# Layer 2's context keys: turned by VectorE in 32x32 blocks and stored in runs of 32 keys, instead of transposed by TensorE

## The chip, the cores and the metric

The kernel runs on one core of one Trainium2 chip. Four compute engines work beside each other, each on its own list of instructions, in order: TensorE (PE in the profile; its weight loads are a second row, PEld), VectorE (DVE), ScalarE (ACT) and GpSimd (POOL). A fifth, SyncE (SP), issues most of the transfers; ScalarE and GpSimd issue some too. All transfers share 16 DMA engines. Work tiles lie in on-chip memory of 128 partitions; TensorE writes its products to a small accumulator memory (PSUM), from which VectorE or ScalarE must copy them.

The metric is the device time of one launch in microseconds (us). Three runs of the kernel before the change took 2389.08, 2390.23 and 2396.24 us; the median is 2390.23.

## The reference, cut to what matters

Four layers, each a cross attention over a context and a feed-forward block, are applied to x of shape 4 x 256 x 256; the context has 4 x 1601 x 256 numbers. The change lies in layer 2's attention, with 16 query heads and 4 key/value heads of 128 numbers:

```python
q = rms_norm((x @ wq).reshape(B, L, 16, 128), q_norm_w)
k = rms_norm((x @ wk).reshape(B, L, 4, 128), k_norm_w)
k_ctx = rms_norm((h_ctx_kv @ wk_ctx).reshape(B, T, 4, 128), k_norm_w)
v_ctx = (h_ctx_kv @ wv_ctx).reshape(B, T, 4, 128)
...
k_full = jnp.concatenate([k_ctx, k], axis=1)
scores = jnp.einsum('blhd,bmhd->bhlm', q, k_full) * scale + mask
probs = jax.nn.softmax(scores, axis=-1)
```

For each of 4 batches and 4 key/value heads, which makes 16 units, 1601 context keys and values are computed from the context, the keys are divided by their root mean square and multiplied by a weight of 128 numbers, and the scores need them turned: the 128 numbers of a key on partitions, the keys side by side. These keys and values do not depend on x.

## The kernel before, in words

**The early pieces.** Because layer 2's context keys and values do not depend on x, they are computed during layers 0 and 1, in pieces that a generator (`l2_early`, L1272) hands out. `fill(n)` (L174) asks for n pieces, at places where TensorE would otherwise wait for a router's small operations or for gathered rows. A unit has seven product pieces (`products`, L1295): two blocks of 128 context rows each, multiplied by a 256 x 256 weight (keys and values at once), copied by ScalarE from the accumulator into `kr_early` (keys) and `va_early` (values, seven buffers), the values sent to device memory (`vd`, L1316) from SP. Every other piece ScalarE squares four blocks of keys and VectorE sums the squares (L1325, L1326). After the seventh, `norm` (L1328) multiplies the unit's keys by the reciprocal root, four operations of up to 512 columns, on GpSimd, or on VectorE while `self.scaler` is set to it (in the adds of layers 0 and 1, where GpSimd is gathering).

Then follow, for the unit before it, four turn pieces (`turns`, L1336): up to four 128x128 transposes by TensorE into the accumulator, one ScalarE copy that multiplies by the key weight (there a column, one number per partition) into `kT_early`, and one transfer from SP to `kd` in device memory, laid out as 128 partitions x 13 blocks x 128 keys. In all 16 x 7 + 16 x 4 = 176 pieces.

**Where they are asked for.** Three in layer 0's attention; `F0` in layer 0's router (L410 on); `G0` nine times in layer 0's adds (`l0_add`, L608); `F1` before layer 1's feed-forward; `G1` in layer 1's adds (L959 on); `LN2`, `Q2`, `C2` while layer 2's first unit is prepared (L1670 on); what is left is then drawn at once. In layer 0's adds GpSimd gathers, for each of eight groups of tokens, eight tiles of expert outputs (L630) into 24 buffers; VectorE adds each, scaled, to x (L622, in written order), and after every second group runs layer 1's small attention (`l1_xattn`).

**What sets the order.** The program is written as one sequence; a planner then orders each engine's list by priority and its own estimates of durations, keeps the dependencies with semaphores and frees buffers. `pin` (and `mm` while `strict` is set) keeps an instruction in written order. At run time each engine, and SP with its transfers, takes its list strictly in order, so an instruction that waits holds up all behind it.

**Layer 2's attention.** The early tiles' memory (`e2`) is freed and used by the attention's probabilities (`p2`, eight buffers) and turned probabilities (`pT2`). `prep` (L1452) loads a unit's keys and values from `kd` and `vd` a unit ahead and adds the 256 own keys. The scores of 32 queries (`scores`, L1549) are made as four matmuls beside each other, one for each 32 of the 128 array columns: matmul a takes keys 32a to 32a+31 of every block, so before the change it reads 32 keys, skips 96, and so on. That lets VectorE turn the probabilities in 32x32 blocks (L1613).

Layer 3 already has keys in such runs: `l3_spread` (L1841) turns them by VectorE and sends them by four transfers.

## Time and profile before

| | us |
|---|---|
| median of three runs | 2390.23 |
| the profiled execution | 2387.69 |
| its span, first to last instruction | 2386.0 |
| TensorE busy | 2255.6 |
| VectorE busy | 1473.2 |
| ScalarE busy | 1272.4 |
| GpSimd busy | 948.7 |

The profile is of one execution. A group is all instructions of one line, engine and shape: its busy time, the mean duration in ns, then the time for which its engine stood idle just before them, with what ended that. "issue" is a wait that the profile can lay to nothing. Matmuls follow each other in a pipeline, so a mean duration is longer than the step from one to the next, and each fp32 product is recorded as two matmuls. The granted clock is TensorE's share of full speed. A wait is laid to what ended last.

The places of the early pieces in that execution: layer 0's attention to 121 us, its router to 208, its experts to 364, its adds (with layer 1's first pieces) to 510, layer 1's feed-forward to 619, its adds to 653, the preparation of layer 2 to 692, then layer 2's attention to 1700.

### The profile page before, as it was taken

The page shows a single profiled execution, that of the slowest core. Times are in us where ns is not written, and L with a number is a line of the kernel's source. Part 1 is how long each engine was busy: PE and PEld are TensorE (multiplying, and loading weights), DVE is VectorE, ACT ScalarE, POOL GpSimd, SP SyncE. Part 2 cuts the span into 40 slices and gives each one's busy share as a digit, 9 for nine tenths or more (in the row PEclk, how much of TensorE's full clock was granted, in tenths as well). Part 3 has the DMA queues.
Part 4 walks back from the last instruction along what each step waited for, and adds up shares of the span by engine and source line. Part 5 has one row for each costly group of instructions (what it writes and reads, how often), then busy time and mean ns, then how long its engine had stood idle before and what let it go on. Part 6 is the DMA issues. An engine that isn't in the chain of part 4 may idle for free.

```text
span 2386.0 us, 42230 instructions
## 1 busy us (share of the span) xinstructions
PE 2255.6 (95%) x14335; PEld 1382.2 (58%) x14335; DVE 1473.2 (62%) x3553; ACT 1272.4 (53%) x2877; POOL 948.7 (40%) x1707
## 2 busy tenths in 40 slices
PE   8989997889989999999999999999899889999996
PEld 5677875777745555555555655555665533444332
DVE  5453532773457777777777777777334574758344
ACT  3334443552474555555555555553232577888994
POOL 1014655503335544555554555554121253334220
PEclk9989998989999999999999999999899999999998
DMA  7165575652550111111111111100534353434320
GB/s 267 41 201 161 172 156 157 197 185 65 167 179 32 43 51 47 47 51 51 51 52 51 51 51 50 44 10 10 205 124 117 114 156 103 109 94 103 83 64 19
DMA packets 156078, 234.47 MB, mean 98 GB/s; under 512 B 33929, under 2 KB 122761, under 8 KB 154666
## 3 DMA queue, kind: packets, MB, share of 16 engines
q1 hardware_dynamic: 138998, 190.07, 25.0%
q0 software_dynamic: 11280, 31.60, 5.4%
q10 hardware_dynamic: 5588, 10.09, 1.4%
q8 instruction: 117, 1.92, 0.3%
q14 instruction: 95, 0.78, 0.1%
HBM read 169.94 MB, written 61.74 MB: 97 GB/s over the span
## 4 chain that ended last, share of the span: by engine, by line
PE 78%; DVE 7%; issue 5%; DMA 4%; ACT 2%; POOL 2%; SPq 1%; ACTq 0%; POOLq 0%; DVEq 0%
PE o L117 17%; PE s L117 17%; PE o L77 6%; PE b L77 3%; PE f2gu L117 3%; PE s L77 3%; PE f1gu L117 2%; PE fill L1307 2%; PE f0gu L117 2%; PE acc L117 2%; PE tpq L117 2%; PE av L117 2%; PE f0y L117 2%; PE f2y L117 1%; PE f1y L117 1%
## 5 line engine op out<-in xcount | busy, mean ns | idle before, releaser
L1572 ACT ACTIVATE p<-s,nmsm 128x448 f32<-128x448 f32 (+2 forms) x512 | 324.7, 639 | 369.6 <-DVE nmsm L1567 317.4
L117 PE MATMUL o<-pT,va 128*128 128x256 f32 (+2 forms) x1920 | 431.7, 377 | 3.3 <-DVE pT L1613 2.9
L117 PE MATMUL s<-kT,qT 128*32 128x448 f32 (+2 forms) x4096 | 424.2, 550 | 4.2 <-ACT p L1572 4.2
L77 ACT ACTIVATE e<-s 128x1024 f32<-128x1024 f32 (+1 forms) x416 | 392.4, 1041 | 57.4 <-PE s L77 56.3
L117 PEld LDWEIGHTS o<-pT,va 128*128 128x128 f32 (+1 forms) x1920 | 344.7, 190 | 127.9 <-issue 75.4
L1607 POOL TENSOR_SCALAR p<-p,rm 128x448 f32<-128x448 f32 (+2 forms) x512 | 320.7, 649 | 6.3
L1567 DVE TENSOR_REDUCE nmsm<-s 128x1 f32<-128x448 f32 (+4 forms) x384 | 293.2, 783 | 4.4
L1613 DVE STREAM_TRANSPOSE pT<-p 128x448 f32<-128x448 f32 (+4 forms) x384 | 278.1, 778 | 11.1 <-POOL p L1607 11.1
L117 PEld LDWEIGHTS s<-kT,qT 128*32 128x32 f32 x4096 | 121.7, 109 | 250.2 <-issue 213.9
L77 PE MATMUL o<-e,va 128*32 128x512 f32 x1656 | 246.9, 614 | 12.3 <-DVE os L77 12.2
L1600 POOL TENSOR_TENSOR rm<-em,tot 32x8 f32<-32x8 f32 x256 | 50.3, 197 | 335.6 <-DVE tot L1597 303.3
L1564 DVE TENSOR_TENSOR s<-s,mask 128x64 f32<-128x64 f32 (+4 forms) x384 | 92.5, 260 | 128.5 <-PE s L117 82.4
L77 PEld LDWEIGHTS s<-qb,kb 32*128 32x128 f32 (+1 forms) x1664 | 65.5, 180 | 182.3 <-issue 143.7
L1307 PE MATMUL fill<-wkc_early,ctxT 128*128 128x256 f32 (+1 forms) x444 | 110.5, 401 | 8.9 <-ACT va_early L1315 6.7
L522 POOL DMA_INDIRECT f0xr<-f0xd,f0src x95 | 91.3, 961 | 66.5 <-PE f0y L117 25.5
L77 PE MATMUL s<-qb,kb 32*128 32x256 f32 (+1 forms) x1664 | 111.5, 331 | 3.1 <-ACT e L77 1.8
L77 POOL CAST kb<-kf 128x384 fp32r<-128x384 f32 (+1 forms) x126 | 65.5, 549 | 96.4 <-PE s L77 61.8
L1307 PEld LDWEIGHTS fill<-wkc_early,ctxT 128*128 128x128 f32 (+1 forms) x444 | 87.0, 200 | 25.3 <-ACT va_early L1315 7.8
L1572 ACT ACTIVATION_READ_ACCUMULATOR p<-s,nmsm 128x1 f32 x512 | 100.5, 196 | 0.0
L1326 DVE TENSOR_REDUCE ss_early<-sq_early 128x4 f32<-128x512 f32 x64 | 37.1, 580 | 82.8 <-ACT sq_early L1325 72.0
L630 POOL DMA_INDIRECT f0yt<-f0yd,f0slot x64 | 63.1, 987 | 60.7 <-DVE x L622 29.8
L117 PE MATMUL f2gu<-f2wgu,f2xsT 128*128 x176 | 85.1, 608 | 0.6 <-ACT f2xsT L114 0.3
(579 smaller groups left out, 3689.2 us busy)
## 6 DMA issues: line engine op xcount, KB each, us to landing
kf<-kd SPq DMA_DIRECT2D x384, 48.0 KB
vd<-va_early SPq DMA_DIRECT2D x96, 128.0 KB
kd<-kT_early SPq DMA_DIRECT2D x48, 256.0 KB
kT<-kd SPq DMA_DIRECT2D x16, 768.0 KB
va<-vd SPq DMA_DIRECT2D x16, 768.0 KB
kd<-kt SPq DMA_DIRECT2D x96, 128.0 KB
f0yd<-f0ys SPq DMA_DIRECT2D x95, 128.0 KB
ctxT<-in_ctxT SPq DMA_DIRECT2D x5, 1664.0 KB
```

What stands on the lines that cost most here:

```text
L77: ins = f(*a, **kw)
L117: self.ordered(self.nc.tensor.matmul(out, lhsT, rhs, start=start, stop=stop, **kw))
L522: nc.gpsimd.indirect_dma_start(out=t, out_offset=None, in_=xd[:, :], in_offset=bass.IndirectOffsetOnAxis(ap=src[:, n : n + 1], axis=0),)
L630: nc.gpsimd.indirect_dma_start(out=yt, out_offset=None, in_=yd[:, :], in_offset=bass.IndirectOffsetOnAxis(ap=slot[:, t, r : r + 1], axis=0),)
L1307: ins = nc.tensor.matmul(tp[:rows, t, :], ctxT[u // NKV2][:, k, c0 : c0 + rows], w[u % NKV2][:, k, :], start=k == 0, stop=k == 1,)
L1326: nc.vector.tensor_reduce(ss[:, m0:m1], sq[:, : m1 - m0, :], AX.X, ALU.add)
L1564: nc.vector.tensor_tensor(sv, sv, mask[:, e0:e1, : nt - CT, :].rearrange("p n t i -> p n (t i)"), ALU.add)
L1567: nc.vector.tensor_reduce(ms[:, 0, e0:e1], s[:, n0:n1, : nt * 32], AX.X, ALU.max, negate=True)
L1572: nc.scalar.activation(p[:, n, : nt * 32], s[:, n, : nt * 32], AF.Exp, bias=ms[:, 0, e : e + 1], accum_out=ms[:, 1, e : e + 1],)
L1600: nc.gpsimd.tensor_tensor(r[32 * a : 32 * a + 32], e[:, a], tot, ALU.mult)
L1607: nc.gpsimd.tensor_scalar(p[:, n, : nt * 32], p[:, n, : nt * 32], r[:, e : e + 1], 1.0, ALU.mult, ALU.mult)
L1613: self.pin(nc.vector.transpose(pT[:, 2 * c + n0 : 2 * c + n1, :nt, :].rearrange("p n t i -> p n (t i)"), p[:, n0:n1, : nt * 32],))
```

## The change

- The keys are no longer transposed by TensorE. `turn` lets VectorE transpose 32x32 blocks of up to five key blocks at a time (`TURNS2`: blocks 0-3, 4-7, 8-12), straight from `kr_early` into `kT_early` (now three buffers). A 32x32 transpose leaves each group of 32 numbers of a key on the partitions of its own group of 32 keys; four transfers a turn, each from 32 partitions, put the pieces where they belong.
- In device memory and on chip the keys now lie as 128 partitions x 4 groups x 13 blocks x 32 keys, so that matmul a of the scores reads one unbroken run.
- The key weight is now a row over 128 numbers on all partitions; it is multiplied in `norm`. On VectorE that is one fused instruction for each of 13 blocks; on GpSimd it is a second pass, in all six operations.
- The turns are no pieces of their own: those of the unit before go into products 3, 4 and 5 of the next unit. That leaves 112 pieces, and `F0`, `G0`, `F1`, `G1` and `C2` ask for fewer.
- The own keys of a unit go into the new layout by two copies instead of one.

```diff
@@ -45,12 +45,13 @@
 CT2 = NM - 1
 
 
-F0 = [0, 0, 0, 0, 6, 8, 4, 4]
-G0 = 9
+F0 = [0, 0, 0, 0, 5, 6, 3, 3]
+G0 = 5
 REGS = 4
-F1 = [1, 2, 2, 3]
-G1 = [7, 4, 4, 3, 2, 2, 2, 2, 2, 2, 0]
-LN2, Q2, C2 = 2, 2, 6
+F1 = [1, 1, 2, 2]
+G1 = [5, 3, 3, 2, 2, 2, 2, 1, 1, 1, 0]
+LN2, Q2, C2 = 2, 2, 4
+TURNS2 = ((0, 4), (4, 8), (8, NM))
 FIRST3 = [7, 1, 3]
 EARLY = B * NKV2
 NH3, HD3 = 32, 8
@@ -1277,14 +1278,18 @@
         nc, tc, i = self.nc, self.tc, self.i
         e2 = self.e2
         self.scaler = nc.gpsimd
-        kw = self.const.tile([P, 1], F32, name="kw_early")
-        nc.sync.dma_start(kw, i["l2_knw"].rearrange("o p -> p o"))
+        kw = e2.tile([P, HD2], F32, name="kw_early")
+        nc.sync.dma_start(kw, i["l2_knw"].to_broadcast([P, HD2]))
         w = []
         for g in range(NKV2):
             w.append(e2.tile([P, 2, 256], F32, name="wkc_early", bufs=NKV2))
             nc.sync.dma_start(w[g], i["l2_wkc"][g])
         self.early_kv = [
-            [self.dram.tile([P, NM, HD2], F32, name=f"{n}{u}", bufs=1) for n in ("kd2", "vd2")] for u in range(EARLY)
+            (
+                self.dram.tile([P, 4, NM, 32], F32, name=f"kd2{u}", bufs=1),
+                self.dram.tile([P, NM, HD2], F32, name=f"vd2{u}", bufs=1),
+            )
+            for u in range(EARLY)
         ]
 
 
@@ -1327,33 +1332,42 @@
 
         def norm(kr, ss):
             self.rstd(ss, ss, 1.0 / HD2, self.eps6)
-            for m in range(0, NM, 4):
-                n = min(4, NM - m)
-                self.scaler.tensor_tensor(
-                    kr[:, m : m + n, :], kr[:, m : m + n, :], ss[:, m : m + n, None].to_broadcast([P, n, HD2]), ALU.mult
+            if self.scaler is nc.vector:
+                for m in range(NM):
+                    nc.vector.scalar_tensor_tensor(kr[:, m, :], kr[:, m, :], ss[:, m : m + 1], kw, ALU.mult, ALU.mult)
+                return
+            for m0, m1 in TURNS2:
+                to = [P, m1 - m0, HD2]
+                for by in (ss[:, m0:m1, None].to_broadcast(to), kw[:, None, :].to_broadcast(to)):
+                    nc.gpsimd.tensor_tensor(kr[:, m0:m1, :], kr[:, m0:m1, :], by, ALU.mult)
+
+        def turn(u, kr, m0, m1):
+
+
+            n = m1 - m0
+            tt = e2.tile([P, 4, (NM - 8) * 32], F32, name="kT_early", bufs=3)[:, :, : n * 32]
+            nc.vector.transpose(
+                tt.rearrange("p r (m i) -> p r m i", i=32), kr[:, m0:m1, :].rearrange("p m (r j) -> p r m j", j=32)
+            )
+            for a in range(4):
+                k = (n - (a == 3 and m1 == NM)) * 32
+                nc.sync.dma_start(
+                    self.early_kv[u][0][:, a, m0:m1, :].rearrange("(r j) m i -> j r (m i)", j=32)[:, :, :k],
+                    tt[32 * a : 32 * a + 32, :, :k],
                 )
-
-        def turns(u, kr):
-            for m in range(0, NM, 4):
-                n = min(4, NM - m)
-                tp = self.take().rearrange("p (n e) -> p n e", n=4)
-                for t in range(n):
-                    nc.tensor.transpose(tp[:, t, :], kr[:, m + t, :], self.ident)
-                kT = e2.tile([P, 4, P], F32, name="kT_early", bufs=4)
-                nc.scalar.activation(kT[:, :n, :], tp[:, :n, :], AF.Copy, scale=kw)
-                nc.sync.dma_start(self.early_kv[u][0][:, m : m + n, :], kT[:, :n, :])
-                yield
 
         def all():
             last = None
             for u in range(EARLY):
-                for kr, ss in products(u):
+                turns = list(TURNS2) if last is not None else []
+                for n, (kr, ss) in enumerate(products(u)):
+                    if n > 1 and turns:
+                        turn(*last, *turns.pop(0))
                     yield
                 norm(kr, ss)
-                if last is not None:
-                    yield from turns(*last)
                 last = (u, kr)
-            yield from turns(*last)
+            for t in TURNS2:
+                turn(*last, *t)
 
         return all()
 
@@ -1454,11 +1468,11 @@
 
                 b = u // NKV2
                 va = two.tile([P, NK, HD2], F32, name="va2", bufs=3)
-                kT = two.tile([P, NK, P], F32, name="kT2")
+                kT = two.tile([P, 4, NK, 32], F32, name="kT2")
                 kd, vd = self.early_kv[u]
-                for t, d in ((kT, kd), (va, vd)):
-                    nc.sync.dma_start(t[:, :CT, :], d[:, :CT, :])
-                nc.sync.dma_start(kT[:, CT, :96], kd[:, CT, :96])
+                nc.sync.dma_start(kT[:, :3, :NM, :], kd[:, :3])
+                nc.sync.dma_start(kT[:, 3, :CT, :], kd[:, 3, :CT, :])
+                nc.sync.dma_start(va[:, :CT, :], vd[:, :CT, :])
                 nc.sync.dma_start(va[:96, CT, :], vd[:96, CT, :])
                 if u % NKV2 == 0:
                     self.xb = turned(b)
@@ -1529,11 +1543,10 @@
                 tp = ps.tile([P, 4, P], F32, name="tpk", tag="tp")
                 for m in range(2):
                     nc.tensor.transpose(tp[:, m, :], ko[:, m, :], self.ident)
-                c = CT * P + 96
-                nc.gpsimd.memset(kT[:, NK - 1, 96:], 0.0)
-                nc.scalar.copy(
-                    kT.rearrange("p m k -> p (m k)")[:, c : c + S], tp[:, :2, :].rearrange("p m k -> p (m k)")
-                )
+                nc.gpsimd.memset(kT[:, 3, NK - 1, :], 0.0)
+                own = tp[:, :2, :].rearrange("p q (j i) -> p j q i", i=32)
+                nc.scalar.copy(kT[:, :3, CT + 1 :, :], own[:, 1:])
+                nc.scalar.copy(kT[:, 3, CT : CT + 2, :], own[:, 0])
                 yield
                 res.extend((kT, va, qT))
 
@@ -1555,7 +1568,7 @@
                     for a in range(4):
                         self.mm(
                             s[32 * a : 32 * a + 32, n, : nt * 32].rearrange("p (t i) -> p t i", i=32),
-                            qT[:, h, q0 : q0 + 32], kT[:, :nt, 32 * a : 32 * a + 32], True, True,
+                            qT[:, h, q0 : q0 + 32], kT[:, a, :nt, :], True, True,
                         )
                 p = main.tile([P, 2, NK * 32], F32, name="p2", bufs=8)
                 for n0, n1, nt in spans(c):
```

The pieces asked for before and after: layer 0's attention 3 and 3, router 34 and 26, layer 0's adds 81 and 45, layer 1's norms 8 and 6, layer 1's adds 30 and 22, preparation 10 and 8, left over 10 and 2.

## The prediction, made before the change was run

> **What bounds the kernel now.** I read the page's first part first, for the busiest engine; then a table of stages, cut where the work changes; then the chain and the waits of the one stage in which TensorE is not busy; then the groups, for prices.
>
> ```profile
> PE 2255.6 (95%) x14335; PEld 1382.2 (58%) x14335; DVE 1473.2 (62%) x3553; ACT 1272.4 (53%) x2877; POOL 948.7 (40%) x1707
> ```
>
> TensorE is the bound over the whole span, so work taken off it is worth asking about. The stages (start:end, length, busy us and instructions of PE, PEld, DVE, ACT, POOL; granted clock; DMA share):
>
> ```profile
> 121.00:208.00 87.00, 80.87 (x386) 67.25 (x385) 41.17 (x126) 33.07 (x84) 15.28 (x18) 0.90 0.56 177
> 208.00:364.00 156.00, 146.25 (x853) 127.00 (x852) 70.94 (x215) 68.90 (x289) 91.47 (x96) 0.99 0.66 171
> 364.00:510.00 146.00, 117.25 (x544) 96.97 (x542) 88.25 (x217) 68.79 (x197) 63.15 (x64) 0.89 0.58 184
> 619.00:653.00 34.00, 32.89 (x166) 28.63 (x165) 18.03 (x49) 20.27 (x56) 13.85 (x14) 1.00 0.71 217
> 653.00:692.00 39.00, 30.85 (x141) 21.90 (x143) 19.42 (x52) 25.75 (x64) 16.38 (x19) 0.92 0.70 239
> 692.00:1700.00 1008.00, 997.99 (x6703) 586.17 (x6696) 768.67 (x1672) 514.99 (x1426) 506.19 (x1127) 0.99 0.14 46
> ```
>
> They are: layer 0's router, its experts, its adds, layer 1's adds, the way into layer 2's attention, that attention. The early pieces run in all but the second and last. In the adds of layer 0 TensorE works 117 of 146 us; the waits of that stretch (engine, line, releaser; total, times, longest) say what the rest is:
>
> ```profile
> DVE ss_early L1326 <- ACT sq_early L1325: 38.6, 8, 11.0
> POOL f0yt L630 <- DVE x L622: 29.8, 13, 10.8
> PE fillg L1307 <- issue: 17.1, 12, 2.9
> ACT kr_early L1314 <- remote: 14.0, 2, 11.5
> ```
>
> PE waits for nothing that the profile shows (383 to 404 us and 448 to 460 us in the timeline, one matmul every 1.4 us or more). Both stretches begin some 11 gathers into an unbroken row of GpSimd's gathers (24 from 370 us, 16 from 437 us) and end 3 us after its last; I call it the gather stall. VectorE meanwhile waits in order for sums of squares that hang on stalled pieces, and with it the adds.
>
> The prices, by form:
>
> ```profile
> L117 PE MATMUL s<-kT,qT 128*32 128x448 f32 x2048 | 221.0, 543 | 4.2 <-ACT p L1572 4.2
> L117 PE MATMUL tpq<-wq,xT 128*128 128x512 f32 x128 | 60.4, 594 | 0.0
> L1613 DVE STREAM_TRANSPOSE pT<-p 128x480 f32<-128x480 f32 x64 | 40.6, 635 | 0.0
> L1613 DVE STREAM_TRANSPOSE pT<-p 128x960 f32<-128x960 f32 x64 | 73.3, 1146 | 5.4 <-POOL p L1607 5.4
> L622 DVE SCALAR_TENSOR_TENSOR x<-f0yt,f0gate,x 128x256 f32<-128x256 f32 x64 | 30.8, 482 | 1.3
> ```
>
> **The change, part by part.** A product piece holds TensorE 1.73 us (timeline: eight matmuls from 365.76, the next eight from 367.49), a unit of seven 11.24 us, so 1.61 us a piece. Four transposes of a turn hold it 0.44 us (377.43 to 377.86), thirteen 1.42 us, so 0.36 us a turn. All 208 transposes are 22.7 us of PE and 64 ScalarE copies (37 us seen). The pieces, counted from the lists (p products, t turns): router 25p+9t to 26p; layer 0's adds 50p+31t to 45p; layer 1's norms 6p+2t to 6p; layer 1's adds 20p+10t to 22p; into layer 2 8p+12t to 10p. PE thus loses 1.6, 19.2, 0.7, 0.4 and 1.1 us.
>
> VectorE gains per unit: three block transposes. By the rows 480 and 960 wide (0.635 and 1.146 us) 512 costs 0.67 and 640 0.80, so 2.1 us a unit. Where VectorE norms, thirteen fused multiplies of 128x128 replace four (2.15 us from 392.51): no such row; from below 0.20 us each (0.30 us of a 128x128 tensor_tensor less some 0.1 of overlap), from above 0.48 (the 128x256 row). I take 0.25, near the shape's own row: 3.3 us, 1.2 more. So 3.3 us a unit. Where GpSimd norms, two passes replace one: 3.4 us becomes 7.
>
> *Router.* PE is busy 81 of 87 and VectorE's one-hots of 155 us wait for PE until 173.8 behind pieces, so PE's 1.6 us count; the waits for the scaling copies (1.8 and 2.0 us on fill) go too, and VectorE's 6.3 us of turns have 46 us of room. Taken -3 (between -5 and +2, should turns stand among the router's own small operations).
>
> *Experts.* The fourth unit's norm lies here among gathers: POOL 3.50 us more. Gathers come every 1.25 us against a tile's 1.44, so most is caught up: +1.5 (0 to +3.5).
>
> *Layer 0's adds.* Before: 365.8 + 91.7 of pieces + 10.4 of layer 1's first eight, which ran here too, + 34 of stall + 6 of small waits = 508, and the next stage's transposes begin at 510.4. PE sets this stage. With 72.5 and 9.7 it ends at 488: -20. But VectorE, busy 88 us, loses 0.7 units (4.7 us each with sums, root and norm) and gains 6.4 times 3.3: 106 us in 126. It has done some 8 us by its first add at 408 us, after the first stall; 98 us from there without one wait end at 506, which is no gain. So PE says -20 and VectorE about 0. I take the middle, -10 (-25, if adds that hang on fewer pieces go into the stall too, to +16, the longer stall of rival B). A transpose on VectorE stands before adds in order, and POOL's next gathers wait for those adds.
>
> *SP and the DMA engines.* 64 transfers become 192; four kd<-kt issues of layer 3 take 1.84 us, so 0.46 each: 5.5 us a unit beside seven value transfers of 0.42, 8.4 us against 11.24 of PE. SP waits in order for VectorE's turns, and behind it stand the value transfers that free seven buffers, a whole unit's. Cover holds while VectorE is less than a unit late; beyond, each us late costs one. Taken +3 (0 to +10). Packets shrink from 2 KB to 512 B. 2100 to 2300 us has 21311 packets of 763 B in 31.3% of 16 engines, 47 ns each; 800 to 1600 us 12129 of 3 KB, 142 ns. So a unit goes from 43 to 64 engine-us, 1.3 us on 16: here the share rises from 0.58 to about 0.64, with room left: zero, up to those 1.3 us a unit if gathers wait for it.
>
> The Trainium skill, "DMA: Bandwidth & Descriptors", Rules for kernel authors, speaks against this: use 128 partitions and coalesce, since transfers under 64 KB are mostly overhead. By its fixed 2 us per transfer three more in a row would be an estimated 6 us a turn; the four issues in 1.84 us above are pipelined. "VectorE: DVE Perf Modes", The three transpose paths, has 390 ns on TensorE and 311 on VectorE for a bf16 128x128, by which the move would gain an estimated 16 us of engine time; our rows, 0.109 against 0.17 us, say it costs engine time and only shifts it.
>
> *Layer 1's norms and adds.* -0.7 in the first, whose VectorE is busy 45 of 109 us. In the second PE loses 0.4 and VectorE gains 3.1 units, 10 us, in 34 of which it fills 18, though 643 to 663 is dense: +1 (-1 to +5).
>
> *Into layer 2.* 13 transposes of the last unit wait for GpSimd (1.9 us) and precede the scores at 691; both go, with twelve copies (7.0 us) on a ScalarE busy 26 of 39, whose lateness PE awaited 4.7 us. Two more products are in PE's 1.1. Against it: the last norm ends 3.5 us later, near 693.5, its turns at 696, its transfers (5.5 us of SP) near 703. The attention's first tiles reuse that memory: probabilities are first written at 695.7, their turned form at 712.3. Taken -4 (-7 to +7, if the first probabilities wait).
>
> *The attention.* Score matmuls read runs that follow each other instead of one run in four. 32 take 3.31 us, eight groups of four, 453 columns on average: 0.91 ns a column; the unbroken 512 of tpq 0.92 (60.4/128). Zero; the attended values' 0.90 bounds it, 5 us either way. The own keys' copy becomes two, ScalarE being half idle; loads come a unit (62 us) ahead. Zero, and it would be a us per unit at most if late.
>
> Sum: -3 +1.5 -10 +3 -0.7 +1 -4 = -12.2. The profiled execution took 2387.7 us (span 2386.0 and 1.7 around it), 2.5 below the median 2390.2: 2375.5 there, 2378 as a median.
>
> **The rivals.** *A: the cover wins.* VectorE paces layer 0's adds and the work moved to it is given back there: 0 instead of -10, in all -2.2, 2388. For: from 465 to 510 us it works over nine tenths; against: it idles 58 of 146 us over the stage. *B: the gather stall grows, slower.* With five pieces a step instead of nine, the first add stands behind 10 pieces (done at 383) instead of 16, so POOL gets its buffers back without its 8.4 us wait and the row of gathers goes on. Unbroken, 64 gathers run from 370 to 450 and the stall from 383 to 453: 70 us instead of 34. Then 365.8+72.5+9.7+70+6 = 524, +16 instead of -7 with SP's 3, in all +10.8, 2401. It decides once the stall grows by the 20 us that PE is spared, 16 gathers. Against: in-order VectorE blocks the row again by itself. *C: PE paces everything*, the full -20 there and none of SP's 3: 2365. *D: the change does nothing* on the path because pieces only fill idle PE: 2390; against it, the sum to 508 above.
>
> **How the numbers follow.** Forecast 0.40, C 0.15, A with D 0.25, B 0.20. 0.3% (7 us) is about what a measurement of this kernel can tell from no change. The forecast's own range is 2369 to 2386; C reaches 2356 with the better bounds of the router and of layer 2's start, B 2409 with the worse. Leaving out a tenth on each side gives 2359 to 2402. Faster: C, and most of the forecast: 0.50; slower: B and the tail of A: 0.24; same 0.26.
>
> **What would show it.** No transposes at L1341's place on PE, 48 block transposes of some 0.7 us on VectorE; PE's busy sum down 20 us or more; layer 0's adds near 136 us instead of 146, with "issue" gaps on PE still near 34 us; the first scores some 4 us sooner after layer 1; attention within 5 us. A stage of 126 us speaks for C, 146 with VectorE over 90% for A, 160 with "issue" near 70 for B. I am wrong if the list that the planner makes for VectorE or SP puts the turns ahead of the adds or the router's operations, or if probabilities wait for the early memory.

## The result: slower by about one per cent

Four runs of the changed kernel took 2411.69 to 2424.65 us, median 2417.14; four of the kernel before, beside them, 2389.08 to 2396.24, median 2391.36. The ratio is 1.0107, with a 95% interval of 1.0072 to 1.0143: slower by some 26 us. The forecast was 2378 (2359 to 2402), so the time lies outside the range, on the slow side, and beyond the slow rival.

The profiled execution took 2411.69 us (span 2410.0), 24.0 more than the one before. The first line of the page's first part for the changed kernel:

```profile
PE 2246.0 (93%) x14127; PEld 1365.9 (57%) x14127; DVE 1521.3 (63%) x3682; ACT 1241.8 (52%) x2825; POOL 985.9 (41%) x1721
```

The 208 transposes are gone, but TensorE's busy sum fell by 9.6 us and not by 22.7; VectorE has 48 us more, GpSimd 37 us more. Where the 24 us came from, by the same milestones in both traces (first or last matmul of each kind):

| from, to | before | after | difference | forecast |
|---|---|---|---|---|
| router's first transposes to experts' first hidden rows | 94.6 | 98.1 | +3.5 | -3 |
| experts | 149.4 | 153.2 | +3.8 | +1.5 |
| layer 0's adds, to layer 1's first transposes | 145.4 | 146.7 | +1.3 | -10 |
| layer 1's norms and feed-forward | 109.1 | 107.7 | -1.4 | -0.7 |
| layer 1's adds, to layer 2's first transposes | 34.1 | 44.4 | +10.3 | +1 |
| to the first score | 37.5 | 28.8 | -8.7 | -4, with the next |
| first score to the second unit's first exponential | 55.7 | 70.9 | +15.2 | |
| from there to layer 2's router | 947.7 | 946.7 | -1.0 | 0 |
| the rest | | | +1.0 | 0 |

The forecast's +3 for SyncE and the DMA engines belongs to no one row. Layer 1's adds and the way to the first score are best read together: product matmuls moved from the second to the first (from 136 to 188 records in the one, from 56 to 32 in the other), so that from layer 1's last product to the first score it is 71.6 us before and 73.2 after.

The table by stage, cut at these milestones (columns as in the prediction's):

```profile
120.60:218.70 98.10, 80.97 (x379) 65.96 (x377) 52.27 (x141) 32.86 (x87) 35.91 (x31) 0.93 0.63 189
218.70:371.90 153.20, 144.82 (x840) 126.05 (x841) 70.66 (x213) 67.43 (x279) 87.23 (x91) 0.98 0.68 164
371.90:518.60 146.70, 105.88 (x396) 82.17 (x396) 103.26 (x285) 49.91 (x151) 77.67 (x70) 0.80 0.64 184
626.30:670.70 44.40, 41.50 (x190) 35.12 (x188) 38.00 (x118) 25.57 (x75) 20.31 (x20) 1.00 0.76 225
670.70:699.50 28.80, 15.37 (x60) 10.61 (x60) 15.78 (x27) 11.50 (x30) 18.52 (x17) 0.82 0.42 118
699.50:770.40 70.90, 58.34 (x381) 27.17 (x381) 44.96 (x97) 32.35 (x91) 26.33 (x59) 0.88 0.28 90
```

The router and the start of attention (first and last row) in the kernel before, cut in the same way:

```profile
121.00:215.60 94.60, 84.01 (x401) 69.38 (x400) 42.78 (x130) 37.04 (x93) 21.02 (x23) 0.90 0.59 187
691.10:746.80 55.70, 51.48 (x375) 23.56 (x375) 41.76 (x92) 32.24 (x88) 25.44 (x59) 0.96 0.16 57
```

In the adds of layer 0 TensorE is busy 106 us, not 116, in a stage as long as before. GpSimd has 36 us in the router, not 21. In layer 1's adds VectorE has 38 us, not 18. In the start of attention TensorE idles 12.6 us, not 4.2.

The waits of layer 0's adds (371.9 to 518.6 us) that answer to those shown of before:

```profile
ACT kr_early L1319 <- remote: 26.1, 4, 10.6
DVE ss_early L1331 <- ACT sq_early L1330: 16.2, 7, 5.4
DVE ss_early L1331 <- ACT va_early L1320: 15.5, 2, 14.4
ACT sq_early L1330 <- DVE ss_early L1331: 14.0, 8, 5.2
PE fill L1312 <- ACT va_early L1320: 13.3, 4, 6.4
PE filly L1312 <- issue: 10.1, 11, 2.9
POOL f0yt L631 <- DVE x L623: 7.8, 6, 3.5
```

Before its sums of squares VectorE waits 32 us for ScalarE (the two rows on `ss_early`) where it waited 44 (38.6 and 5.6), and GpSimd waits 8 us for the adds where it waited 30. TensorE's waits at "issue" add up to 15.4 us in this list and to 23.8 in the one before: the stall is there and no longer than it was. What is new on TensorE is the wait for ScalarE's copies of values, 13.3 us against 2.0; ScalarE in turn waits 14.0 us for VectorE's sums before it squares, against 4.4.

The prices were about right. By form, the same kernel:

```profile
L118 PE MATMUL s<-kT,qT 128*32 128x448 f32 x2048 | 222.8, 542 | 0.0
L1337 DVE SCALAR_TENSOR_TENSOR kr_early<-kr_early,ss_early,kw_early 128x128 f32<-128x128 f32 x117 | 33.0, 348 | 0.1
L1349 DVE STREAM_TRANSPOSE kT_early<-kr_early 128x512 f32<-128x512 f32 x32 | 21.9, 699 | 12.1 <-POOL kr_early L1342 12.1
L1349 DVE STREAM_TRANSPOSE kT_early<-kr_early 128x640 f32<-128x640 f32 x16 | 13.3, 831 | 7.7 <-POOL kr_early L1342 7.7
```

The turns take 0.70 and 0.83 us (forecast 0.67 and 0.80), the thirteen fused multiplies 13 x 33.0/117 = 3.7 us a unit (forecast 3.3), the score matmuls 542 ns (543 before). What the forecast did not have stands at the ends of the turns' lines: 19.8 us in which VectorE, in order, waits for GpSimd's norm before a turn. The place where it costs, in VectorE's timeline of the changed kernel (start, length):

```profile
195.91 1.77 DVE L503 TENSOR_TENSOR f0rows<-f0lane,f0place 128x1024 f16<-128x1024 f16 x1
200.47 2.04 DVE L503 TENSOR_TENSOR f0rows<-f0lane,f0place 128x1024 f16<-128x1024 f16 x1
...
215.36 0.71 DVE L1349 STREAM_TRANSPOSE kT_early<-kr_early 128x512 f32<-128x512 f32 x1 [5.15 <-POOL kr_early L1342]
217.80 0.71 DVE L1349 STREAM_TRANSPOSE kT_early<-kr_early 128x512 f32<-128x512 f32 x1 [1.73 <-POOL kr_early L1342]
218.44 0.38 DVE L575 TENSOR_TENSOR f0h<-f0h,f0gu 128x96 f32<-128x96 f32 x2
```

The last line is the first expert's own work. It stands behind two turns that wait 5.15 and 1.73 us for GpSimd, and TensorE waits 3.53 us for it. At the entry of layer 2 the same thing happens on GpSimd, whose timeline reads:

```profile
686.81 1.26 POOL L1342 TENSOR_TENSOR kr_early<-kr_early,ss_early 128x512 f32<-128x512 f32 x1 [1.46 <-DVE ss_early L127]
...
690.61 2.25 POOL L1342 TENSOR_TENSOR kr_early<-kr_early,ss_early 128x512 f32<-128x512 f32 x2
692.82 2.75 POOL L1342 TENSOR_TENSOR kr_early<-kr_early,kw_early 128x512 f32<-128x512 f32 x2
695.53 2.04 POOL L1530 TENSOR_TENSOR qo<-qo,rq 128x512 f32<-128x512 f32 x2
```

The scaling of the first queries (last line) follows the last unit's norm, and TensorE's transposes of these queries wait 10.4 us for it. Behind the first scores another wait follows: TensorE waits 9.4 us for the second unit's query weights.

```profile
PE tpqT L1540 <- POOL qo L1530: 10.4, 1, 10.4
PE tpq L118 <- DMA wq<-in_l_wq: 9.4, 1, 9.4
```

SyncE's list shows why the weights are late:

```profile
698.96 13.45 SPq L1354 DMA_DIRECT2D kd<-kT_early  x12
712.51 0.39 SPq L1458 DMA_DIRECT2D wq<-in_l_wq  x1
```

After the first four of these twelve transfers SyncE waits 7.9 us for VectorE's turns. GpSimd's norm had ended at 695.6, but the last two turns start only at 708.0: in VectorE's list they stand behind the masks of the first scores, for which VectorE itself waits 12.1 us.

### The profile page after: what moved, and what is told of

The parts are those of the page before. It is cut to its first block, busy times and chain, and to the rows that moved or that the text cites. A ratio compares the mean times of both kernels' runs of the same rounds, so it can differ in the third digit from the quotient of the medians.

```text
span 2410.0 us, 41957 instructions
## 1 busy us (share of the span) xinstructions
PE 2246.0 (93%) x14127; PEld 1365.9 (57%) x14127; DVE 1521.3 (63%) x3682; ACT 1241.8 (52%) x2825; POOL 985.9 (41%) x1721
## 4 chain that ended last, share of the span: by engine, by line
PE 75%; DVE 9%; issue 5%; DMA 4%; POOL 4%; ACT 2%; SPq 1%; ACTq 0%; DVEq 0%; POOLq 0%
PE o L118 17%; PE s L118 17%; PE o L78 6%; PE b L78 3%; PE f2gu L118 3%; PE s L78 2%; PE tpq L118 2%; PE acc L118 2%; PE f1gu L118 2%; PE f0gu L118 2%; PE av L118 2%; PE fill L1312 2%; PE f0y L118 2%; PE f2y L118 1%; POOL kr_early L1342 1%
## 5 line engine op out<-in xcount | busy, mean ns | idle before, releaser
L78 PE MATMUL o<-e,va 128*32 128x512 f32 x1656 | 246.7, 613 | 12.3 <-DVE os L78 12.2
L1312 PE MATMUL fill<-wkc_early,ctxT 128*128 128x256 f32 (+1 forms) x452 | 117.9, 412 | 24.2 <-ACT va_early L1320 18.6
L523 POOL DMA_INDIRECT f0xr<-f0xd,f0src x95 | 91.2, 960 | 59.9 <-PE f0y L118 23.2
L631 POOL DMA_INDIRECT f0yt<-f0yd,f0slot x64 | 70.1, 1096 | 45.2 <-DMA vd<-va_early 16.1
L78 PEld LDWEIGHTS o<-e,va 128*32 128x32 f32 x1656 | 40.6, 108 | 76.0 <-issue 36.9
```

Source lines behind the costliest of these rows:

```text
L78: ins = f(*a, **kw)
L523: nc.gpsimd.indirect_dma_start(out=t, out_offset=None, in_=xd[:, :], in_offset=bass.IndirectOffsetOnAxis(ap=src[:, n : n + 1], axis=0),)
L631: nc.gpsimd.indirect_dma_start(out=yt, out_offset=None, in_=yd[:, :], in_offset=bass.IndirectOffsetOnAxis(ap=slot[:, t, r : r + 1], axis=0),)
L1312: ins = nc.tensor.matmul(tp[:rows, t, :], ctxT[u // NKV2][:, k, c0 : c0 + rows], w[u % NKV2][:, k, :], start=k == 0, stop=k == 1,)
```

## The experiments

Each run stands beside the kernel before on the same chip, and ratios are to that. The chips differ: on two of them the kernel before takes 2339 to 2340 us, on the others 2388 to 2396. Stages are therefore compared between runs of like chips. The changed kernel itself ran only on the slower sort (ratios 1.0107 and, in e5, 1.0127); on the faster sort e2, which equals it up to layer 2, stands in for it in the early stages.

### Where does the time go: e1 to e4 (faster sort of chip)

**e1: all norms on VectorE.**

```diff
-            if self.scaler is nc.vector:
+            if True:
                 for m in range(NM):
                     nc.vector.scalar_tensor_tensor(kr[:, m, :], kr[:, m, :], ss[:, m : m + 1], kw, ALU.mult, ALU.mult)
                 return
```

> The changed kernel with one edit: all sixteen units' norms run on VectorE (13 fused operations of about 0.25 to 0.35 us), none on GpSimd. Theory H (a VectorE turn that stands in VectorE's in-order list waits for GpSimd's two-pass norm, and the layer's own VectorE work stands behind it): in the changed kernel VectorE's turns wait 14.0 us for GpSimd in the router stage and 4.1 us among the experts, where PE then waits 3.9 us for f0h, and the query scaling of the first attention unit waits about 10 us behind a norm on GpSimd. Then the experts start about 3 us sooner, end about 7 us sooner, and the first queries are there 5 to 10 us sooner; the end 8 to 15 us below the changed kernel, some 2397 to 2404 in the profile. Rival V (VectorE is simply too full in these stages, 4 us more per unit): 8 units leave GpSimd for VectorE, the waits for GpSimd go, but the stages stay as long or grow; the end 0 to 8 us above the changed kernel. Rival S (only the SP queue at the start of attention counts): the early stages gain, the first attended value stays within 3 us of 740, the end within 4 us.

Measured: 1.0076 (1.0049 to 1.0103). The router took 91.2 us against 101.3 in e2, the way from layer 2's first transposes to the first queries 19.4 against 25.9, the experts 145.5 against 145.4. First score to first attended value took 42.0 us (40.5 in the changed kernel), so nothing was gained there. Below are the router's stage in e2, the same in e1, and VectorE's wait for GpSimd in e2's router; e1 has no such wait.

```profile
120.20:221.50 101.30, 85.04 (x379) 69.13 (x377) 52.35 (x141) 32.50 (x87) 35.81 (x31) 0.86 0.61 184
```

```profile
120.60:211.80 91.20, 79.34 (x379) 65.36 (x378) 60.67 (x193) 32.26 (x86) 9.10 (x9) 0.93 0.66 200
```

```profile
DVE kT_early L1349 <- POOL kr_early L1342: 10.0, 6, 4.2
```

VectorE has 8 us more work there and the stage is 10 us shorter. Theory H holds in router and entry; rival V falls there. Among the experts nothing was gained, which H did not expect.

**e2: the second unit's loads ahead of the last unit's transfers.**

```diff
+            w, kept1 = load(1), keys(1)      # keys(u): the four loads that prep(u) began with
             for _ in self.early:
                 pass
             self.es2.close()
...
-                            w = load(g1)
-                            pieces = prep(n + 1, w, ready)
+                            if n:
+                                w = load(g1)
+                            pieces = prep(n + 1, w, ready, None if n else kept1)
```

> The changed kernel with one edit: the loads of the second attention unit (its query weights, turned keys and values) are issued on SP ahead of the last unit's twelve key transfers, which wait for VectorE's turns. Nothing is added or taken away. Theory S (these loads stand behind transfers that wait in SP's in-order queue; PE's second unit of queries then waits 9.4 us for its weights): the first attended value comes 9 to 13 us sooner (740 to about 729), and so does the end, about 2400 in the profile. Rival H (GpSimd's norm and VectorE's list hold the start of attention up, and the weights are only the last of several): the wait for the weights goes, another of the same length takes its place, the end moves by less than 4 us.

Measured: 1.0166 (1.0141 to 1.0191), slower still. The wait for wq is gone, but first score to first attended value grew to 47.8 us. With the weights there, the planner put the second unit's squares and copies ahead of the first exponentials in ScalarE's list: the first exponential came 26.7 us after the first score (5.5 in the changed kernel), and TensorE waited 9.4 us for exponentials. Theory S was not tested cleanly; e7 does that.

**e3: one turn and four transfers a unit.**

```diff
-TURNS2 = ((0, 4), (4, 8), (8, NM))
+TURNS2 = ((0, NM),)        # GpSimd's norm keeps its three parts
...
-            tt = e2.tile([P, 4, (NM - 8) * 32], F32, name="kT_early", bufs=3)[:, :, : n * 32]
+            tt = e2.tile([P, 4, NM * 32], F32, name="kT_early", bufs=1)[:, :, : n * 32]
```

> The changed kernel with one edit: each unit is turned by one VectorE operation over all 13 blocks and stored by four transfers, not by three operations and twelve transfers: 64 key transfers in all instead of 192, the same bytes and the same layout. Theory S-count (the number of transfers on SP costs, at 0.46 us each): 128 fewer transfers take 59 us off SP's queue; at the start of attention the last unit's four transfers take about 2 us instead of 13 and the second unit's weights come some 8 us sooner; the end 5 to 12 us below the changed kernel. Rival (the waits for GpSimd's norm and for VectorE decide, not the count): one long turn of about 2 us waits for the whole norm, with the layer's VectorE work behind it; the end within 4 us of the changed kernel or above it. Either way a third fewer packets would say nothing of the adds if their length stays at 147 us within 2 us.

Measured: 1.0086 (1.0059 to 1.0113), 5 to 10 us less than the changed kernel's ratios give. The first score came 22.6 us after layer 2's first transposes (28.8 after the change), and the wait for wq was gone. S-count is met in size, but not by its mechanism: first score to first attended value still took 40.3 us, the first scores came sooner because TensorE's wait for the first queries fell from 10.4 to 3.5 us, and the adds of layer 0 (114.9 against e2's 117.8) moved little. The Trainium skill ("DMA: Bandwidth & Descriptors", Rules for kernel authors) says to coalesce many small transfers into a large one. If each of the 128 transfers saved had cost the page's fixed 2 us in a row, that would be an estimated 256 us; the gain here is 5 to 10 us, and e11 below finds none for the count alone.

**e4: turns two pieces later.**

```diff
-                    if n > 1 and turns:
+                    if n > 3 and turns:
```

> The changed kernel with one edit: the three turns of a unit stand behind the fifth, sixth and seventh piece of the next unit instead of the third, fourth and fifth, so GpSimd's norm has two pieces (some 5 us) longer before VectorE comes to its turn. Theory H (VectorE's turns wait for GpSimd's norm, layer work behind them): the 14.0 us that VectorE waits for GpSimd in the router stage fall below 5, the 4.1 us among the experts go, the experts end 4 to 7 us sooner and the end is 4 to 8 us below the changed kernel; the start of attention, where the last unit has no next one, stays as it is. Rival (that wait is slack, the router stage is paced by PE and the vector chain): the wait goes and the stage stays within 1 us.

Measured: 1.0117 (1.0091 to 1.0142), no gain. Among the experts VectorE's wait fell from 4.1 to 0.5 us and the stage to 143.2 (145.4 in e2), as H said. In the router VectorE still waited 11.8 us. The line in the source doesn't place the turn: the planner does, and there it put the turns where GpSimd's norm was still running.

### Chips and rivals: e5 to e8 (slower sort)

**e5 and e6: both kernels again.**

> The changed kernel itself, beside the experiments, because the first four experiments took some 2 per cent less than both kernels' first runs, and their layer-0 adds took 113 to 118 us and not 147, without the 28 us in which PE waited at the label issue while rows were being gathered. If that stall comes and goes with the chip and not with the edits, this run's layer-0 adds take 113 to 119 us as well, its span is 2360 to 2368, and its ratio to the kernel before 1.008 to 1.014. If the edits took it away (fewer transfers, no GpSimd norm), the adds take 140 us or more here and the span is above 2385.

> The kernel before, for one profile beside the experiments. Theory V (where the gather stall is gone, PE paces the adds before the change and VectorE after it): the layer-0 adds take 98 to 110 us with PE busy over 95 per cent, VectorE under 85 per cent; the first attended value stands about 28 us behind the first score. Rival (something else than the adds made this chip's runs short): the adds take over 130 us.

Measured: e5 1.0127 (1.0102 to 1.0153), layer 0's adds 147.9 us; e6 146.8 us. Taken literally, e5's expectation says that the first four edits had removed the stall. But this chip was one where the kernel before takes 2394 us, and e7 and e8 there had the stall too, while e2 had not, which does the same as the changed kernel until layer 2. TensorE's waits in the adds of e2 list no piece that waits at "issue":

```profile
PE fill L1312 <- ACT va_early L1320: 16.1, 4, 6.6
PE tp_ln L192 <- issue: 11.4, 1, 11.4
```

So the stall that the prediction gave 34 us to goes with the chip, not with the edits. What it is stays open. The losses by milestone in e5 against e6 repeat the first pair's within 5 us each.

**e7: e2's loads, with ScalarE's order held.** ScalarE's operations of the first unit are pinned in the order in which they are written, on top of e2's edit.

```diff
+            act = InOrder(nc.scalar, self.pin)      # from the first unit's scores on; nc.scalar again from the second
...
-                        nc.scalar.activation(
+                        act.activation(
```

> The changed kernel with the second unit's loads ahead of the last unit's key transfers, as in the run before that made the start of attention 7 us longer, and with ScalarE's work of the first unit (exponentials, squares, copies of the query preparation) held in the order in which it is written, so that the second unit's preparation can't go ahead of the first exponentials in ScalarE's list. Theory S (waiting for wq costs 9 us, and the earlier run only put another order in its place): first score to first attended value falls from 40 to 28 to 32 us, the end 8 to 12 us below the changed kernel. Rival H (the start of attention is long because VectorE and GpSimd still have the last unit to finish): over 37 us, the end within 4 us of the changed kernel.

Measured: first score to first attended value 33.2 us (42.1 in e5), near theory S's 28 to 32. The end gained less: median 2421.58 against 2425.53, ratio 1.0112 (1.0095 to 1.0129), whose interval overlaps e5's. Of the 8.9 us, 2.7 come back in the rest of attention (981.1 us from there to layer 2's router, 978.4 in e5). The wait for wq is real; what its repair alone is worth in the end isn't clear of the noise.

**e8: every turn of layer 0's adds twice.**

```diff
-            nc.vector.transpose(
+            for _ in range(1 + self.doubled):       # True in l0_add alone
+                nc.vector.transpose(
```

> The changed kernel with every turn of the layer-0 adds done twice into the same tile (some 20 turns of 0.74 us, 14.5 us of VectorE more); nothing else changes. Theory V (VectorE paces the layer-0 adds after the change): the adds grow by 10 to 15 us, and the end by as much. Rival P (PE, the gathers or the transfers pace them, VectorE has room): the adds grow by less than 4 us.

Measured: 12.1 us more turns on VectorE (26.6 against 14.5), the adds 157.3 us against 147.9, the median 2435.10 against 2425.53. With 9.4 of 12.1 us passed on, VectorE has hardly any room in this stage: theory V, and the prediction's rival A, in their mechanism.

### Adding repairs, moving pieces: e9 to e11

(Slower sort.) **e9** is e1 and e7 together; **e10** is e9 with five pieces taken out of layer 1's adds; **e11** is e9 with e3's one turn and four transfers. e10's edit:

```diff
-F0 = [0, 0, 0, 0, 5, 6, 3, 3]
+F0 = [0, 0, 0, 0, 6, 7, 4, 3]
-G1 = [5, 3, 3, 2, 2, 2, 2, 1, 1, 1, 0]
+G1 = [5, 3, 2, 1, 1, 1, 1, 1, 1, 1, 0]
-LN2, Q2, C2 = 2, 2, 4
+LN2, Q2, C2 = 2, 2, 6
```

> The changed kernel with all norms on VectorE (run e1) and the second attention unit's loads ahead of the last unit's transfers with ScalarE's order held (run e7). Theory H+S (two separate causes: VectorE's turns and the first queries wait for GpSimd's two-pass norm in the router stage, among the experts and at the entry of layer 2, worth 0.4 to 0.5 per cent; and SP's in-order queue at the start of attention, worth some 9 us): the gains add up, 15 to 20 us, ratio to the kernel before 1.003 to 1.007; first score to first attended value 28 to 34 us. Rival (both repair the same wait): no more than the better one alone, ratio 1.007 to 1.011.

> The kernel of the run before it with five early pieces taken out of layer 1's adds (22 to 17), three put into the norms of the router stage (17 to 20) and two into the preparation of layer 2 (4 to 6). Theory PE (PE paces layer 1's adds: 41 of 43 us busy, 52 matmul records more than before the change, and has 12 us of idle time in the router stage and 7 us in the preparation): the stage from layer 1's last product to layer 2's first transposes falls by 8 to 10 us (42 to 33), the router grows by 0 to 4 us, the preparation by 0 to 3, the end 2 to 8 us below the run before it. Rival (VectorE, with 37 of 43 us, or the vector chains of router and preparation set these stages): the sum of the three stages stays within 2 us.

> The kernel of run e9 with one turn and four transfers for each unit instead of three and twelve. With the norm on VectorE a turn waits for no other engine, so theory S-count (the number of transfers costs in itself, 128 on SP at 0.46 us) expects 3 to 7 us below e9; the rival (in run e3 the gain came from the turn standing later and whole, not from the count) expects within 2 us of e9.

Measured: e9 1.0045 (1.0030 to 1.0061), e10 1.0058 (1.0041 to 1.0076), e11 1.0038 (1.0024 to 1.0052). The two repairs add up, as H+S said, as far as the intervals can tell. e10's layer-1 adds fell by 5.4 us (47.1 to 41.7), but the router grew by 4.9 and the time didn't fall: the rival, no gain from moving pieces. e11 is within 2 us of e9: with all norms on VectorE and the second unit's loads ahead, the count of transfers has no effect that can be seen.

### Taking parts out: e12 to e16

**e12 leaves out the turn** (faster sort; the keys are stored unturned, in the same transfers). **e13 leaves out GpSimd's second pass** (same chip; the key weight is missing in the units normed there).

```diff
-            tt = e2.tile([P, 4, (NM - 8) * 32], F32, name="kT_early", bufs=3)[:, :, : n * 32]
-            nc.vector.transpose(...)
+            tt = kr[:, m0:m1, :].rearrange("p m d -> p (m d)").rearrange("p (r x) -> p r x", r=4)
```

```diff
-                for by in (ss[:, m0:m1, None].to_broadcast(to), kw[:, None, :].to_broadcast(to)):
+                for by in (ss[:, m0:m1, None].to_broadcast(to),):
```

> The changed kernel with VectorE's 48 turns left out: the four transfers of each piece read the normed keys as they lie, in the same sizes and number, so the keys of layer 2 are stored unturned (the computation is changed by that). Theory V+H (the turns cost twice: 14.5 us of VectorE in the layer-0 adds, where doubling them made the adds 9 us longer, and VectorE's waits for GpSimd's norm in the router stage and among the experts): the layer-0 adds fall by 5 to 9 us, router and experts together by 4 to 8 us, the end 12 to 20 us below the changed kernel, ratio to the kernel before 1.003 to 1.007. Rival N (GpSimd's and VectorE's longer norm and the new deal of pieces cost the time, the turn itself is cheap): less than 6 us, ratio above 1.009.

> The changed kernel with GpSimd's second pass left out, which multiplies the normed keys by their weight (the units normed on GpSimd go without the weight; the computation is changed by that); VectorE's norms stay. GpSimd's norm falls from about 7 to 8 us for each unit to about 4, as it was before the change. Theory H (what hurts is how long GpSimd's norm keeps VectorE's turns and the first queries waiting): VectorE's wait for GpSimd in the router stage falls from 14 to below 6 us, router and experts fall by 4 to 7 us together, the first queries of layer 2 come 3 to 6 us sooner, ratio to the kernel before 1.007 to 1.009. Rival (the waits go, the stages are paced by something else): ratio 1.010 to 1.013.

Measured: e12 1.0048 (1.0030 to 1.0065), e13 1.0067 (1.0045 to 1.0089). Against e2, the router fell from 101.3 to 86.6 us without turns and to 86.4 with the shorter norm: either end of the wait pays, and more than was expected. But layer 0's adds took 114.2 and 113.3 against 117.8, so e12 missed its 5 to 9 us there; doubling the turns costs, taking them off gains little. The stage that differs most is layer 1's adds (e12, then e13):

```profile
573.40:605.50 32.10, 32.10 (x150) 27.97 (x149) 23.02 (x77) 18.27 (x55) 18.20 (x16) 1.00 0.79 236
```

```profile
575.20:620.80 45.60, 42.95 (x190) 36.48 (x189) 38.79 (x118) 25.08 (x75) 20.92 (x20) 0.96 0.75 224
```

Without the turns VectorE has 23 us there and the stage ends 12 us sooner; TensorE does 40 product matmuls fewer in it than in e2 and 40 more between it and the first score, which takes no longer for it (29.2 us, 28.8 in e2). TensorE's 41 of 44 us in the changed kernel were thus no bound. In that kernel VectorE waits less than 7 us in the whole stage, and the chain that leads to layer 2's first transposes runs mostly over its norms, turns and adds; the pieces fill the time until then.

**e14 leaves out all the added work**: no turn, no weight, the norm's four operations and one pass as before the change, four transfers. **e15 is the whole changed kernel with its product pieces put back** towards where they were; **e16 is e14 with e15's deal.** All three ran on one chip.

```diff
-            self.fill(G0)
+            self.fill(G0 + (t < 3))
-G1 = [5, 3, 3, 2, 2, 2, 2, 1, 1, 1, 0]
+G1 = [5, 3, 2, 1, 1, 1, 1, 1, 1, 0, 0]
-LN2, Q2, C2 = 2, 2, 4
+LN2, Q2, C2 = 2, 2, 7
```

> The changed kernel with all work left out that the change added, and its deal of pieces kept: no turns, no key weight, the norm as before the change (four operations on either engine, one pass), four transfers for each unit (the computation is changed by that: keys unturned and unweighted). TensorE's 208 transposes stay gone. Theory W (the added work carries the whole loss, and the freed 20 us of TensorE would be a gain if nothing took their place): faster than before, ratio 0.992 to 0.998. Rival D (the new deal of the pieces loses time by itself, by 52 matmul records more in layer 1's adds): ratio 1.000 or above.

> The whole changed kernel with its product pieces put back where they were before the change: three more into the layer-0 adds, six fewer in layer 1's adds (22 to 16), three more in the preparation of layer 2. Theory W (the deal is neutral: the work moves and the stages' bounds with it, as in run e10): ratio within 0.003 of the changed kernel's 1.011 to 1.013. Rival D: layer 1's adds fall from 44 to 48 us to 35 to 38 and the rest stays, ratio 1.005 to 1.008.

> Run e14 with the deal of run e15: only products are left, dealt as before the change. Theory W: within 0.002 of e14. Rival D: 0.003 to 0.006 below e14, and it is here that the kernel gets faster than before, ratio 0.992 to 0.998.

Measured: e14 0.9956 (0.9940 to 0.9973), e15 1.0134 (1.0110 to 1.0157), e16 0.9969 (0.9959 to 0.9979). In neither pair does the deal move the time by more than 0.3%. That tests only part of the old deal, though: in e15's trace the planner put 414 product matmuls into layer 0's adds (394 after the change, 432 before) and 172 into layer 1's adds (188 and 136).

The added work is worth 1.0134 - 0.9969, 1.65% or 39 us. The stages show where. These are the router and layer 0's adds, in e15 and then in e16:

```profile
120.90:220.80 99.90, 83.73 (x379) 68.03 (x376) 52.31 (x141) 32.55 (x87) 35.81 (x31) 0.88 0.62 187
371.60:525.10 153.50, 108.85 (x417) 84.88 (x416) 104.91 (x287) 51.75 (x158) 73.96 (x70) 0.82 0.61 175
```

```profile
120.70:209.10 88.40, 78.41 (x380) 64.96 (x379) 42.84 (x130) 32.56 (x86) 22.83 (x25) 0.94 0.70 213
359.00:500.60 141.60, 102.56 (x381) 80.02 (x379) 85.92 (x210) 47.42 (x147) 69.60 (x68) 0.80 0.57 170
```

It is some 12 us in each of the two, 5.5 from layer 1's last product to the first score, 6.0 from there to the second unit's first exponential, and 3 in all the rest. What the freed TensorE and ScalarE bring is 7 to 11 us by the ratios and no more.

### The turn without what came with it: e17 and e18

**e17** computes the same as the changed kernel and keeps its turns and its deal. The norm is one pass of four operations again. The key weight is multiplied in by GpSimd during attention, on the turned keys, where it is one number a partition. One turn and four transfers serve a unit (e3's edit). **e18** is e17 with e7's edit.

```diff
-            if self.scaler is nc.vector:
-                ...
+            for m in range(0, NM, 4):
+                n = min(4, NM - m)
+                self.scaler.tensor_tensor(
+                    kr[:, m : m + n, :], kr[:, m : m + n, :], ss[:, m : m + n, None].to_broadcast([P, n, HD2]), ALU.mult
+                )
...
                 nc.gpsimd.memset(kT[:, 3, NK - 1, :], 0.0)
+                for part in (kT[:, :3, :NM, :], kT[:, 3, :CT, :]):
+                    nc.gpsimd.tensor_scalar(part, part, self.kw2, 1.0, ALU.mult, ALU.mult)
```

> A version of the changed kernel that computes the same and keeps its turns and its deal, but takes off the other added work: the norm in one pass of four operations, as before the change; the key weight is multiplied in by GpSimd after the turned keys are loaded in attention, where the weight is one number for each partition (two operations, about 2.4 us by the rate of its probability scaling, 16 times, beside PE); one turn and four transfers for each unit. Theory T (the turn itself still costs the 0.5 to 0.7 per cent that leaving it out brought): ratio 1.000 to 1.004. Rival Q (the turn cost what it did because it waited for the two-pass norm and stood in three pieces with twelve transfers; without these it is nearly hidden): ratio 0.995 to 0.999, a kernel faster than both.

> Run e17's kernel with the second attention unit's loads ahead of the last unit's transfers and ScalarE's order held, as in run e7. Theory S (waiting for wq is a cost of its own): 2 to 4 us below e17. Rival (with four transfers for the last unit the wait is gone already, as in run e3): within 2 us of e17 or above.

Measured: e17 0.9957 (0.9942 to 0.9973), 2385.09 us beside 2396.21: faster than both kernels. e18 0.9961 (0.9947 to 0.9975). So rival Q: the turn costs next to nothing when nothing makes it wait; e17's ratio is that of e14, which has no turn and no weight at all, though each was taken on its own chip. Its groups on VectorE (turn, norm) and on GpSimd (weight, norm):

```profile
L1346 DVE STREAM_TRANSPOSE kT_early<-kr_early 128x1664 f32<-128x1664 f32 x16 | 30.4, 1903 | 3.1 <-POOL kr_early L1337 3.1
L1337 DVE TENSOR_TENSOR kr_early<-kr_early,ss_early 128x512 f32<-128x512 f32 (+1 forms) x36 | 19.8, 586 | 0.1
```

```profile
L1545 POOL TENSOR_SCALAR kT<-kT,kw_early 128x1248 f32<-128x1248 f32 (+1 forms) x32 | 30.2, 946 | 5.7 <-DMA kT<-kd 2.6 <-DVE pT L1625 1.2
L1337 POOL TENSOR_TENSOR kr_early<-kr_early,ss_early 128x512 f32<-128x512 f32 (+1 forms) x28 | 25.1, 926 | 83.5 <-DVE ss_early L127 83.5
```

The turns' 30.4 us are nearly the changed kernel's 35.2, but VectorE waits 3.1 us for GpSimd, not 19.8. The 30.2 us of weight lie in attention, where GpSimd is about half idle. e17's router, layer 0's adds and layer 1's adds:

```profile
120.60:206.60 86.00, 78.68 (x379) 64.84 (x377) 47.62 (x132) 32.10 (x87) 19.17 (x21) 0.94 0.68 202
362.90:500.90 138.00, 100.85 (x391) 78.68 (x389) 92.61 (x217) 48.60 (x150) 71.31 (x68) 0.84 0.60 175
606.00:640.80 34.80, 32.68 (x150) 27.68 (x148) 23.58 (x59) 17.89 (x54) 14.92 (x15) 1.00 0.65 200
```

The first and third are 12.1 and 9.6 us shorter than in the changed kernel, whose chip was of the same sort; the second is 8.7 shorter; the experts between them are 3.1 longer (156.3). In e18 the start of attention is 4 us shorter up to the first attended value, the rest of attention is 7 us longer (982.1 against 975.1), and the time is the same; in e17 already TensorE has no wait for wq.

## Why the prediction was wrong

**The sum had the gain too large and the price far too small.** Its -12.2 us are -17.7 of gain and +5.5 of price, some of the price being already inside the middle taken for layer 0's adds. The kernel with the added work left out (e14, e16) gained 7 to 11, and the full gain that rival C counts, 25, isn't there either. The added work costs 39 us, and the sum let nearly all of it vanish under cover. That -12.2 lies near the 7 to 11 is chance: they are not the same quantity.

**Router -3** is the first step that failed. Its room, "VectorE's 6.3 us of turns have 46 us of room", was counted in busy time, and the case of turns among the router's own operations was priced at +2. In the runs a turn brings GpSimd's whole norm with it: VectorE's list is in order, and what stands behind the turn waits as long. The price is 10 us (e1) to 15 us (e12, e13) on the faster sort of chip and 12 us on a slower one (e15 against e16). "3.4 us becomes 7" was fair (7.7 measured), but it was charged among the experts, against gathers, and at the last norm before layer 2, and not in the router.

**Experts +1.5** measured +3.8. The wait of 3.53 us for the first expert's rows is shown; e4 takes 3.6 of VectorE's 4.1 us of waiting away and gains 2.2. The rest isn't settled, since e1 gained nothing there.

**Layer 0's adds -10** measured +1.3. The step "I take the middle" failed: VectorE's estimate, which said 0, was the right one of the two (106 us forecast, 103 measured), and e8 shows its lack of room. The other estimate, -20, was too large by itself: with all added work left out the stage still takes 134.0 us (e14) or 141.6 (e16), against 126 by that sum, and the added work takes the rest back, some 12 us. Rival A had this, with its 2388 too low for the rest. That VectorE alone bounds the stage isn't shown: taking the turns alone out gained at most 4 us where the stall is absent. e17 with 11 us less on VectorE took 138.0. B fell: the stall did not grow.

**Layer 1's adds +1** measured +10.3. Part of that is work that came forward from the next stage; with the way to the first score the two measured +1.6, where the forecast had -3 for them and the start of attention. The added 10 us of VectorE were set against "34 of which it fills 18". But the chain from the adds to layer 2's first transposes runs on VectorE, and its list mixes the early work into it. With the turns out (e12, 32.1 us) or the added work reduced (e17, 34.8) the loss is gone; with e15's deal (43.9) or GpSimd's pass out (e13, 45.6) it stays. From layer 1's last product to the first score, e14 takes 62.9 us and e16 65.1, the changed kernel 73.2 and e15 70.6: the added work costs 6 to 10 us here.

**Into layer 2 -4, attention 0** measured -8.7 and +15.2, in sum +6.5. The first scores came sooner after layer 2's first transposes, but 1.6 us later after layer 1's last product, where the prediction said some 4 sooner; the start behind them grew. The last unit's transfers, said to end near 703, ended at 712.4. The two named dangers were there under other names. Not memory was late: the first queries stood behind the last norm (10.4 us, e1 gains 6.5), and the second unit's weights behind twelve transfers in SyncE's list. The step on SP, +3, looked for lateness of buffers and for the sum of issues; it didn't ask what loads stand behind transfers that wait. e7 takes 8.9 us off up to the first attended value, and less off the end. That scores are read at the same rate and that attention then runs on unchanged (-1.0) was right.

**PE's busy sum down 20 us** measured 9.6. In layer 0's adds TensorE lost 10.4 us where 19.2 were counted: the granted clock was 0.80, before 0.89, TensorE was idle for 28% of the stage, before 20%, and the matmuls of one group took 441 ns on average against 389. In the start of attention it worked 6.9 us more, at a clock of 0.88 against 0.96. That the clock fell because TensorE idled more isn't shown by a run.

## What to carry to other kernels

Work that is moved to an engine with room in its busy time is not free: on an in-order list it brings along every engine that it waits for, and the next stage's own operations wait with it. So cost a moved step by what must be finished before it and by what stands behind it, engine by engine, SyncE's list included. When a change loses, leave its parts out one at a time: here the turn that looked guilty was nearly free once it waited for nothing, and the multiplication that came with it could be done later, on the turned keys, by an engine with time to spare.

## What the hardware showed that was not expected

VectorE's one-hot of 128x1024 numbers of 16 bits takes 0.69 us, but 1.77 and 2.04 us in the two shown above at 195.91 and 200.47; GpSimd's norm ran from 193.53 to 201.96 without a break. In e1, where GpSimd norms nothing, all eight take 0.68 to 0.69. The Trainium skill has this on "SBUF — State Buffer", Who interferes with whom: VectorE and GpSimd share a pair of ports as an exclusive lock. These runs agree in kind; no run here separates the ports from another cause.

Layer 0's adds, with the same work, took 117.8 us on one chip (e2) and 146.7 and 147.9 on two others (the changed kernel), without and with TensorE's waits at "issue" while rows are gathered. The kernel before differs by some 50 us between such chips. No run here shows the cause.
